# First-level sums of W1 and W2 moved to the first row's QKV stage, second-level sums of W1 called over the whole second one

## The chip, the cores and the metric

The kernel runs on one core of a Trainium2 chip. The metric is the time of one execution on the device, in microseconds. Before the change it was 2320.35 us, the median of 3 runs that lay between 2318.24 and 2321.5 us. The numbers of the trace come from one further execution, taken with the hardware profiler.

## What is computed

The reference is one block of a transformer with modulation by a condition (a DiT block), in fp32. x comes as (2, 2048, 512); each of its two rows is one sequence of 2048 tokens with causal attention over 16 heads of 32.

```
mod = silu(condition) @ Wada + bada
sh_a, sc_a, gt_a, sh_m, sc_m, gt_m = split(mod, 6)
xm = layernorm(x, g1, be1) * (1 + sc_a) + sh_a
x  = x + gt_a * attention(xm, Wqkv, Wproj, bproj)       # causal
xm = layernorm(x, g2, be2) * (1 + sc_m) + sh_m
h  = gelu(xm @ W1 + b1)                                 # W1: 512 x 2048
x  = x + gt_m * (h @ W2 + b2)                           # W2: 2048 x 512
```

## The kernel before

**Stages.** The program is written out by hand, stage after stage. A head computes the modulation from Wada and normalises the first tokens. Then come, for row 0, a QKV stage, an attention phase (line 541) and a projection phase (from line 1004); the same three for row 1; and last the MLP of both rows together.

**QKV stage.** `Qkv.run` (line 856) goes through four groups of 512 tokens. A group has 12 steps: eight tiles `ps_qk` of queries and keys and four tiles `ps_v` of values, each four matmuls of 128x512. Ahead of a group, its rows of x are loaded on SyncE (line 781), VectorE takes their statistics (line 215) and normalises them (line 263). Between the matmuls of these steps stand the score matmuls of the first attention units and the maxima that VectorE takes of them (lines 456 and 461). After step n of group g the stage calls `also(g, n)`, which is where the weight sums are put into the program's order. The row 0 stage has its `also` at line 1175, the row 1 stage at line 1228.

**Sums of weights.** The MLP does its two products by a scheme of seven products in place of eight (Strassen's, in Winograd's form), at two levels: seven outer ones of seven inner ones. The weights' side of it is made ahead of the MLP, on GpSimd, with scratch memory in DRAM between the levels.

*First level*, class `Quarters` (line 898). There are 16 pieces, 0 to 7 of W1 and 8 to 15 of W2. `step()` (line 924) issues the store of the piece before, takes a room, issues four loads of 128 KB (line 940) and four sums of 128x256 (line 922); the store (line 911) of 896 KB goes to `w1d` or `w2d`. A room holds one piece; where rooms come in pairs, two pieces share a buffer. Loads, sums and store are all on GpSimd: its DMAs go through the software queue, which is GpSimd's own.

*Second level of W1*, class `FirstLayer` (line 972). It reads `w1d` back, one load of 1024 KB (line 968) for each of seven outer products, makes four sums of 128x512 (line 963), and stores 1792 KB to `w1e` (line 996). Its buffer "w49" has two rooms; the first call issues two loads, and each later call the sums and the store of one room and the load of the next. The second-level sums of W2 are made in the MLP itself. SyncE reads `w1e` in the MLP.

**Where these calls stand before the change.** In the first row's stage the even steps of the last group each call `quarters.step()`: six pieces, 0 to 5. Their rooms are the buffer "wada", one buffer, two pieces to a fill. It holds Wada's last parts before, so it is free only after PE has used them for the last modulation. In the second row's stage the odd steps call `quarters.step()` until the last piece is stored (pieces 6 to 15, in the "w49" buffers), and from there on the even steps call `late.step()`.

**What sets the order.** Each engine works through its instructions in the program's order, and each instruction waits for the data and the buffer that it needs. The calls in `also` place GpSimd's work in GpSimd's own order only: behind the last GpSimd instruction of the code ahead of them, and ahead of the causal selects (line 602) and the sums of exponentials (line 623) of the attention units. Nothing ties a call to the matmul step that it stands behind, except the buffer it has to wait for. In the head GpSimd has two clears and the broadcasts of `bada`; in the QKV stages it has little else than these weight sums. The pool of tiles "qkv0" (variable `qp`) lives as long as the first stage.

Of the kernel before, what the change touches and what calls it, by code (L numbers as in the profile page):

```python
# [8 lines left out]
F32 = mybir.dt.float32  # L9
# [8 lines left out]
P = 128  # L18
# [9 lines left out]
def dit_block_kernel(  # L28
# [39 lines left out]
    C = D // P  # L68
# [5 lines left out]
    MTT = MT // P  # L74
    NG = T // MT
# [8 lines left out]
    def pool(name, bufs=1, **kw):  # L84
        return tc.tile_pool(name=name, bufs=bufs, reuse_waits="tile", **kw)
# [119 lines left out]
    def act(ins):  # L205

        return tc.keep_in_program_order(ins)
# [561 lines left out]
    class Qkv:  # L769
# [41 lines left out]
        def group(self, g, hp, between, among):  # L811
# [32 lines left out]
            for t in range(MTT):  # L844
# [9 lines left out]
                n += 1  # L854

        def run(self, hp, also):

            row = self.row
            for g in range(NG):

                def between(n):
                    if g + 1 < NG:
                        if n == 0 and g + 1 not in self.xts:
                            self.load_x(g + 1)
                        if n in (5, 8):
                            self.norm(g + 1, n // 8)()
                    elif n == 8:

                        row.rows(0)
                        act(nc.scalar.activation(first, eps, AF.Exp))  # L870
                    also(g, n)
# [22 lines left out]
    piece = 7 * C // 2 * P  # L894
# [172 lines left out]
    with pool("wada") as wp, pool("qkv0") as qp, pool(  # L1067
# [16 lines left out]
        def load_wada(s0, s1):  # L1084
            w = wp.tile([P, 2, C, D], F32, tag="wada", name="wada")
            if s0 % 3 == 2:
                mr = modr
            else:
                mr = wp.tile([P, D], F32, tag="mr", name="mr")
                nc.gpsimd.memset(mr, 0.0)  # L1090
            for n, s in enumerate((s0, s1)):
                nc.gpsimd.dma_start(
                    mr[n * HD : n * HD + B, :],
                    bada[s * D : (s + 1) * D].partition_broadcast(B),
                )
            for k in range(C):
                for n, s in enumerate((s0, s1)):
                    nc.sync.dma_start(w[:, n, k, :], wada_v[:, k, s * D : (s + 1) * D])
            wada[s0] = w, mr
# [12 lines left out]
        def modulation(s0):  # L1112

            w, mr = wada.pop(s0)
            ps = ps_sp.tile([P, D], F32, tag="s", name="ps_mod")
            for k in range(C // 2):  # L1120
                for half in range(2):
                    for n in range(2):
                        at = (2 * half + n) * HD
                        kk = half * C // 2 + k
                        mm(
                            ps[at : at + HD, :], sc[:, kk, :], w[:, n, kk, :],
                            start=(k == 0), stop=(k == C // 2 - 1),
                        )

            def columns():  # L1130
                nc.vector.tensor_tensor(mr, ps, mr, ALU.add)
                if s0 % 3 == 2:
                    return
                ps_t = ps_sp.tile([P, C, 2, B], F32, tag="s", name="ps_modt")
                for k in range(C):
                    mm(
                        ps_t[:, k], mr[:, k * P : (k + 1) * P], pickc,
                        start=True, stop=True,
                    )
                nc.vector.tensor_copy(  # L1140
                    mod[:, s0 : s0 + 2], ps_t.rearrange("p c s b -> p s c b")
                )

            return columns

        def scale_shift(a, c, r_g, r_be, shift, scale):

            for dst, r in ((a, r_g), (c, r_be)):
                nc.vector.scalar_tensor_tensor(
                    dst, mod[:, scale], 1.0,  # L1150
                    col(r, C).unsqueeze(2).to_broadcast([P, C, B]),
                    ALU.add, ALU.mult,
                )
            nc.vector.tensor_tensor(c, c, mod[:, shift], ALU.add)
# [17 lines left out]
                modulate((k, k + 1))  # L1172
        act(nc.vector.tensor_copy(pick, pickc.unsqueeze(3).to_broadcast([P, 2, B, P])))

        def also(g, n):

            if g == NG - 1 and n % 2 == 0:
                quarters.step()
            if g == 0 and n == 2:
                load_wada(2, 5)  # L1180
            elif g in (1, 2) and n == 3:
                qkv.columns = modulation(g + 1)
            elif g in (1, 2) and n == 4:
                qkv.columns()
                if g == 1:
                    load_wada(3, 4)
                else:
                    scale_shift(a2, c2, r_g2, r_be2, 3, 4)

        quarters = Quarters()  # L1190
        with pool("hl0") as hp:

            def rooms():

                w = wp.tile([P, 2 * C * D], F32, tag="wada", name="w7")
                return [w[:, k * piece : (k + 1) * piece] for k in range(2)]

            quarters.more_rooms = rooms
            qkv.run(hp, also)
            quarters.store()  # L1200
# [5 lines left out]
    with pool("qkv1") as qp, pool("ps_qkv1", bufs=6, space=PSUM) as ps_mm:  # L1206
        qkv = Qkv(row, qp, ps_mm)
        qkv.xts[0] = past.next_s

        def between(n):  # L1210
            if n == 6:
                qkv.load_w(nc.gpsimd)

            if n < MTT:
                qkv.stats(0, n, True)
            if n in (5, 8):
                qkv.norm(0, n // 8)()
            if n == 8:
                qkv.load_x(1)
            if n >= NT - MTT:  # L1220
                qkv.stats(1, n - (NT - MTT), True)

        project_phase(past, ps_mm, between)

        with pool("hl1") as hp:
            late = FirstLayer(hp)

            def also(g, n):
                if quarters.at <= FC:
                    if n % 2 == 1:  # L1230
                        quarters.step()
                elif n % 2 == 0:
                    late.step()

            def rooms():
                w = hp.tile([P, 7, C * P], F32, tag="w49", name="w7", bufs=2)
                w = w.rearrange("p n d -> p (n d)")
                return [w[:, k * piece : (k + 1) * piece] for k in range(2)]

            quarters.more_rooms = rooms  # L1240
            qkv.run(hp, also)
            assert quarters.at >= FC and late.at == 7 and not late.rooms
# [682 lines left out]
```

## Time and profile before

| what | us |
|---|---|
| median of 3 runs | 2320.35 |
| profiled execution | 2323.13 |
| its span | 2321.4 |
| head, up to the first QKV matmul | 18.46 |
| row 0: QKV stage | 194.99 |
| row 0: attention | 529.0 |
| row 0: projection | 60.4 |
| row 1: QKV stage | 195.5 |
| row 1: attention and projection | 599 |
| MLP | 724 |

The times of the stages are read from the trace, from the first matmul of one stage to the first of the next. The page of the profile gives first the busy time of each engine, then the span in forty slices, the DMA queues, and the chain of work that ended last; a row of the trace tells when an instruction began, how long it took, on what engine and line, out of which tile into which, and in square brackets how long its engine stood idle before it and which engine's result ended that (`<-DVE mx L456`: VectorE's tile mx, made in line 456). A row of a stretch tells begin and end, length, the busy time of PE, its weight loads, VectorE, ScalarE and GpSimd, the granted clock, the busy share of the DMA engines and GB/s. The row of a DMA shows the time of its issue on its queue, and the time to landing is given for a line as a group.

### The profile page before, as it was taken

The numbers are of one execution on the slowest core, as the hardware profiler recorded it, in microseconds if no ns is written. First come the engines' busy times: TensorE is split into PE (matmuls) and PEld (weight loads), VectorE is DVE, ScalarE is ACT, GpSimd is POOL, SyncE is SP. The second block draws the span as 40 slices with busy tenths as digits, with TensorE's granted clock in tenths as the row PEclk, the third lists the DMA queues.
The fourth block names the chain that finished last, engine by engine and source line by source line (L and its number), as shares of the span: only waits on it lengthen the run. The fifth ranks groups of instructions, "written<-read, shape, count | busy, mean of one in ns | idle before, by whom it ended". The sixth has DMA issues, their size and how long they took to land. (4 is left out here: it accounts for less than half of the span.)

```text
span 2321.4 us, 33398 instructions
## 1 busy us (share of the span) xinstructions
PE 2270.8 (98%) x12141; PEld 1388.8 (60%) x12141; DVE 1582.5 (68%) x3117; ACT 914.6 (39%) x1744; POOL 1290.9 (56%) x1036
## 2 busy tenths in 40 slices
PE   8999999999999999999999999999999999999998
PEld 4455545455544444555455554446888888888887
DVE  3366776777666735677667777555896876877787
ACT  2112555555565021155555554622332152251230
POOL 1052987878793663478788886653764602602510
PEclk9999999999999999999999999999999999999999
DMA  7577216151233799981522404265375554654643
GB/s 257 185 243 204 55 28 133 29 119 47 74 115 127 241 297 298 320 235 24 113 48 48 100 24 134 81 206 205 118 279 200 199 186 146 212 173 151 216 143 116
DMA packets 118524, 355.60 MB, mean 153 GB/s; under 512 B 14496, under 2 KB 15052, under 8 KB 103640
## 3 DMA queue, kind: packets, MB, share of 16 engines
q1 hardware_dynamic: 107040, 293.64, 41.9%
q0 software_dynamic: 10944, 59.28, 7.0%
q8 instruction: 96, 1.57, 0.3%
q14 instruction: 68, 0.56, 0.1%
q10 hardware_dynamic: 376, 0.55, 0.1%
HBM read 253.80 MB, written 107.48 MB: 156 GB/s over the span
## 5 line engine op out<-in xcount | busy, mean ns | idle before, releaser
L593 ACT ACTIVATE e<-st 128x512 f32<-128x512 f32 (+1 forms) x1152 | 573.1, 579 | 411.6 <-PE st L203 350.5
L461 DVE TENSOR_REDUCE mx<-s 128x1 f32<-128x512 f32 x604 | 408.0, 687 | 185.0 <-PE s L203 183.6
L623 POOL TENSOR_TENSOR ee<-ee,e 128x1024 f32<-128x1024 f32 x212 | 498.8, 2385 | 8.3 <-ACT e L593 8.3
L203 PE MATMUL s<-kst,qst 128*128 128x512 f32 (+3 forms) x1032 | 466.5, 453 | 15.9 <-DVE mx L461 6.3
L203 PE MATMUL st<-qst,kst 128*128 128x512 f32 (+3 forms) x1280 | 410.1, 387 | 0.0
L203 PE MATMUL ps_a<-sum,room 128*128 128x256 f32 x1504 | 357.4, 382 | 6.6 <-DVE c L1409 3.8
L203 PEld LDWEIGHTS ps_a<-sum,room 128*128 128x128 f32 x1504 | 281.5, 190 | 56.0 <-issue 8.7
L203 PE MATMUL o<-e,vv 128*32 128x512 f32 (+3 forms) x2560 | 300.8, 539 | 0.8 <-POOL e L602 0.8
L203 PEld LDWEIGHTS s<-kst,qst 128*128 128x128 f32 x1032 | 194.5, 189 | 174.0 <-DVE mx L461 58.6
L456 DVE CUSTOM_DVE_ANT_0 junk<-s,causal 128x512 bf16<-128x512 f32 (+3 forms) x428 | 209.2, 489 | 126.2 <-PE s L203 118.7
L203 PEld LDWEIGHTS st<-qst,kst 128*128 128x128 f32 x1280 | 227.5, 188 | 96.8 <-issue 66.7
L623 POOL TENSOR_TENSOR ee<-e 128x1024 f32<-128x1024 f32 x84 | 198.4, 2384 | 130.5 <-ACT e L593 130.4
L203 PE MATMUL ps_qk<-xmT,wqkv 128*128 128x512 f32 x512 | 240.5, 597 | 1.8 <-DVE xmT L263 1.8
L602 POOL TENSOR_SCALAR_AFFINE_SELECT e<-e 128x256 f32<-128x256 f32 x256 | 103.8, 436 | 107.2 <-ACT e L593 74.2
L203 PEld LDWEIGHTS ps_qk<-xmT,wqkv 128*128 128x128 f32 x512 | 94.2, 190 | 97.7 <-issue 91.4
L1637 POOL TENSOR_TENSOR c<-c,h 128x512 f32<-128x512 f32 x40 | 58.2, 1474 | 160.8 <-ACT c L1635 160.8
L203 PE MATMUL ps_b<-sum,room 128*128 128x256 f32 x608 | 143.6, 379 | 0.0
L203 PEld LDWEIGHTS ps_b<-sum,room 128*128 128x128 f32 x608 | 115.0, 190 | 15.4
L203 PE MATMUL ps_v<-wqkv,xmT 128*128 128x512 f32 x256 | 122.3, 594 | 0.0
L203 PEld LDWEIGHTS o<-e,vv 128*32 128x32 f32 x2560 | 60.8, 108 | 101.1 <-issue 83.4
L203 PE MATMUL st<-fold,sel 32*128 32x512 bf16 (+1 forms) x1152 | 116.1, 372 | 3.6 <-DVE mhl L482 2.6
L461 DVE TENSOR_REDUCE mx<-st 128x1 f32<-128x512 f32 x164 | 112.7, 687 | 4.9 <-PE st L203 2.7
(179 smaller groups left out, 2869.6 us busy)
## 6 DMA issues: line engine op xcount, KB each, us to landing
qst<-q SPq DMA_DIRECT2D x128, 256.0 KB
room<-w1e SPq DMA_DIRECT2D x28, 1024.0 KB
kst<-k SPq DMA_DIRECT2D x24, 1024.0 KB
room<-w1e SPq DMA_DIRECT2D x28, 768.0 KB
room<-w2e SPq DMA_DIRECT2D x21, 1024.0 KB
q<-hl SPq DMA_DIRECT2D x32, 512.0 KB
k<-hl SPq DMA_DIRECT2D x32, 512.0 KB
room<-w2e SPq DMA_DIRECT2D x21, 768.0 KB
```

What stands on the lines that cost most here:

```text
L203: return tc.keep_in_program_order(nc.tensor.matmul(*args, **kw))
L456: nc.vector.tensor_tensor_reduce(junk[:, :w], s[:, :w], causal[:, QB - w :], 1.0, MASKED, ALU.add, ALU.max, m,)
L461: nc.vector.tensor_reduce(m, s[:, :w], axis=AX.X, op=ALU.max)
L593: act(nc.scalar.activation(e[:, h % 2, :w], sts[h][:, :w], AF.Exp))
L602: nc.gpsimd.affine_select(d, d, pattern=[[0, 2], [1, P]], compare_op=ALU.is_ge, fill=0.0, base=0, channel_multiplier=-1,)
L623: act(engine.tensor_tensor(dst, x, y, ALU.add))
L1637: nc.gpsimd.tensor_tensor(c, c, piece_of(base, i, t, pair), ALU.add)
```

## The change

Two calls of `also` are rewritten. Neither the tiles nor the sums are changed, only in which room and at which place of GpSimd's order they are made.

In the first row's stage the 48 steps are numbered through (`at`). `free` is 29, the step behind the last modulation's use of Wada. Ahead of it, steps 9, 13, 17, 21 and 25 each make one piece, 0 to 4, in a room of its own from the pool `qp` (tag "w7", one buffer, so piece after piece) and issue its store at once. From step 29 on, each odd step makes a piece, 5 to 14, in the pairs of the "wada" buffer: five fills of it, where there were three. In the second row's stage, one piece is left (15); then `late.step()` is called at each step whose number leaves 2 when divided by 5, nine calls from step 7 on, where it was called at each even step after the pieces.

```diff
+        free = 2 * (C * 2 + MTT) + 5
+
         def also(g, n):
 
-            if g == NG - 1 and n % 2 == 0:
+            at = g * (C * 2 + MTT) + n
+            if at < free:
+                if at >= 9 and at % 4 == 1:
+                    quarters.rooms = [qp.tile([P, piece], F32, tag="w7", name="w7")]
+                    quarters.step()
+                    quarters.store()
+            elif at % 2 == 1:
                 quarters.step()
             if g == 0 and n == 2:
                 load_wada(2, 5)
...
             def also(g, n):
+                at = g * (C * 2 + MTT) + n
                 if quarters.at <= FC:
                     if n % 2 == 1:
                         quarters.step()
-                elif n % 2 == 0:
+                elif at % 5 == 2:
                     late.step()
```

## The prediction

> **What bounds the kernel now.** I read the page first, then the stretches by stage, then the waits and the order in time around the places where the matmul engine stands still.
>
> ```profile
> PE 2270.8 (98%) x12141; PEld 1388.8 (60%) x12141; DVE 1582.5 (68%) x3117; ACT 914.6 (39%) x1744; POOL 1290.9 (56%) x1036
> ```
>
> PE is occupied for 98% of the span of 2321.4 us, so some 50 us of the whole program are open idle time, and the work that the change moves (GpSimd sums of weights and their transfers) is on none of PE's instructions. It can only act where it makes PE wait, or stops PE from waiting. The next table is three of the stretches, with busy time by engine in the order PE, PEld, DVE, ACT, POOL, then granted clock, DMA share and GB/s: the head up to the first QKV matmul, the first row's QKV stage and the second row's.
>
> ```profile
> 0.00:18.46 18.46, 8.09 (x41) 4.76 (x41) 8.69 (x32) 3.68 (x6) 6.17 (x20) 1.00 0.89 300
> 18.46:213.45 194.99, 194.94 (x570) 95.22 (x571) 101.30 (x248) 38.57 (x69) 40.62 (x55) 1.00 0.68 217
> ...
> 802.80:998.30 195.50, 190.74 (x533) 93.80 (x532) 99.65 (x240) 36.85 (x67) 102.47 (x130) 0.99 0.93 310
> ```
>
> The first row's stage loses 0.05 us of PE; the second row's loses 4.76 us and some clock, with DMA at 0.93 instead of 0.68. In order of time, those 4.76 us are two stalls (PE rows), and the second is followed by 3.41 us at half clock (stretch row):
>
> ```profile
> 855.55 0.44 PE L203 MATMUL s<-kst,qst 128*128 128x384 f32 x1 [1.57 <-DVE mx L456]
> ```
> ```profile
> 902.83 0.50 PE L203 MATMUL s<-kst,qst 128*128 128x512 f32 x1 [3.17 <-DVE mx L461]
> ```
> ```profile
> 904.31:907.72 3.41, 3.41 (x7) 1.37 (x5) 1.72 (x4) 0.60 (x1) 0.00 (x0) 0.50 1.08 333
> ```
>
> So the stage has 1.57 + 3.17 + 3.41 x 0.5 = **6.45 us** to give, and no other stage is touched from that side. DVE is named, but DVE itself had waited for the next group's rows of x:
>
> ```profile
> 851.64 0.69 DVE L215 BATCH_NORM_STATS2 stat<-x 128x6 f32<-128x512 f32 x1 [3.27 <-DMA x<-in_x_dram]
> ```
> ```profile
> 842.34 3.18 SPq L781 DMA_DIRECT2D x<-in_x_dram  x4
> ```
>
> x is asked for at 842.34 and its second statistics still wait for it at 851.64, 9.3 us later. It comes late, its statistics and four subtractions then run in one piece, and the maxima of the scores wait behind them on DVE. PE has two banks for scores and stops. Over the stage DVE waits 13.7 us for x, in the first row's stage 2.8 us; that is the measure of how much the software queue's transfers press on SyncE's:
>
> ```profile
> DVE stat L215 <- DMA x<-in_x_dram: 13.7, 6, 4.7
> ```
> ```profile
> DVE stat L215 <- DMA x<-in_x_dram: 2.8, 2, 2.2
> ```
>
> **The change part by part.** Nine of the ten pieces of the second row's stage go to the first row's, and the order on PE, DVE, ACT and SyncE stays the same but for buffers. GpSimd's queue does not look at the clock: its instructions wait only for their own transfers and buffers, wherever the text places the call. Three places matter.
>
> *Head, +1.5 us.* Piece 0 has a room of its own, so its four loads go out right behind GpSimd's first four small ones. Until 18.46 us the DMA engines are busy 0.89, and the head ends on them:
>
> ```profile
> 12.39 0.18 PEld L203 LDWEIGHTS ps_mod<-wada,sc 128*32 128x32 f32 x4 [0.51 <-DMA wada<-in_L_cond_Wada_dram]
> ```
> ```profile
> 18.46 20.87 PE L203 MATMUL ps_qk<-xmT,wqkv 128*128 128x512 f32 x48 [1.78 <-DVE xmT L263]
> ```
> ```profile
> w<-in_L_cond_W_dram POOLq DMA_DIRECT2D x64, 128.0 KB, 5.5
> w1d<-w POOLq DMA_DIRECT2D x8, 896.0 KB, 7.1
> ```
>
> Wada feeds the modulation, which feeds xmT, which releases the first QKV matmul. 4 x 128 KB at the head's 300 GB/s are 1.7 us put in front of the rest of Wada. Bounds: nothing (they land behind Wada) and 2.5 us (at the 204 GB/s of a slow stretch below); I take 1.5. Pieces 1 to 4 follow one by one, each some 14 to 20 us (loads, 4 sums, a store that must land), and are done before 127 us. They fall in a stage at DMA share 0.68 whose DVE waits only 2.8 us for x: 0, at most 2 us if one store meets the x of the third group.
>
> *First attention, +2.6 us.* Pieces 5 to 14 go in five pairs through the room of the Wada buffer, which comes free where it did before. Before, there were three:
>
> ```profile
> 127.29 5.05 POOL L940 DMA_DIRECT2D w<-in_L_cond_W_dram  x7 [108.70 <-DMA kst<-k]
> ...
> 149.96 4.95 POOL L940 DMA_DIRECT2D w<-in_L_cond_W_dram  x7 [4.20 <-DMA w1d<-w]
> ...
> 157.26 2.32 POOL L922 TENSOR_TENSOR w<-w 128x256 f32<-128x256 f32 x3 [0.96 <-DMA w<-in_L_cond_W_dram]
> ...
> 164.16 1.06 POOL L911 DMA_DIRECT2D w1d<-w  x1 [0.30 <-POOL w L922]
> 169.44 4.95 POOL L940 DMA_DIRECT2D w<-in_L_cond_W_dram  x7 [4.22 <-DMA w1d<-w]
> ...
> 185.13 1.07 POOL L911 DMA_DIRECT2D w1d<-w  x1 [1.06 <-issue]
> ```
>
> The pairs start 22.67 and 19.48 us apart, and each must wait until the last pair's stores have landed. The landing of a store (the row is that of line 911 as a group) takes from its issue 4.7 us in quiet stretches, 8.9 in the median:
>
> ```profile
> DMA to landing us min/median/max: 4.7/8.9/12.4
> ```
> ```profile
> 835.98 2.15 POOL L940 DMA_DIRECT2D w<-in_L_cond_W_dram  x4
> ```
>
> The third pair lands at 185.13 + 8.9 = 194.0. A pair in quiet time: the second one took 165.22 - 149.96 = 15.26 us to the end of its last issue. The last pairs are of W2, whose issue takes 2.15 / 4 = 0.54 us against 4.95 / 7 = 0.71, so 8 x 0.17 = 1.4 less; without the 0.96 of waiting it is 12.9. Then 3.6 us to land and 0.6 to the next start. Pair four starts at 194.6, pair five at 211.7 and leaves GpSimd at **224.6**. Behind it in the same queue stand the causal selects of the first attention unit, two of them (2.28 / 6 = 0.38 us each in the row below) ahead of PE's first product with values:
>
> ```profile
> 222.83 1.07 PE L203 MATMUL o<-e,vv 128*32 128x512 f32 x8
> ```
> ```profile
> 1001.13 2.28 POOL L602 TENSOR_SCALAR_AFFINE_SELECT e<-e 128x256 f32<-128x256 f32 x6
> ```
>
> 224.6 + 0.8 + 0.1 of handing over - 222.8 = 2.6 us (after a head of 1.5 both ends move alike). Bounds: 0 if the pairs are 2.6 us quicker, 13.8 if the last two take the first one's 22.67 and 18.5. The key load of the next head group on SyncE now waits for the same room; it needs 27 us at 204 GB/s and its first reader comes at 269.21, so from 228.2 it lands at 255: covered by 14 us, nothing.
>
> ```profile
> 214.00:241.00 27.00, 25.90 (x180) 14.40 (x180) 19.56 (x42) 15.75 (x33) 13.23 (x13) 1.00 0.98 204
> ```
> ```profile
> 269.21 0.22 PE L203 MATMUL s<-kst,qst 128*128 128x128 f32 x1
> ```
>
> The Trainium skill, "TensorE: Matmul & The Clock Gate", section "What's actually happening", puts the fall to half rate after at least one idle window of about 3.4 us. By that rule a stall of 2.6 us costs no clock and the sum stays. The rows above show 3.17 us of idleness followed by 3.41 us at 0.50, and none at 1.57, so the limit here is lower, between the two; if it were passed, 1.7 us more.
>
> *Second QKV stage, -2.2 us.* The second-level rooms are said to be spread, one call in five. But GpSimd runs ahead: before, the seven rooms took from 902.19 to 1000.54, each waiting for the store of the room before.
>
> ```profile
> 902.19 0.59 POOL L968 DMA_DIRECT2D w<-w1d  x1
> ...
> 1000.54 0.58 POOL L996 DMA_DIRECT2D w1e<-w  x1 [0.30 <-POOL w L963]
> ```
> ```profile
> w1e<-w POOLq DMA_DIRECT2D x7, 1792.0 KB, 7.8
> ...
> w<-w1d POOLq DMA_DIRECT2D x7, 1024.0 KB, 7.7
> ```
>
> After the one piece left (2.15 us of issues, a few us of landing, four sums, one store) they start some 10 us into the stage and need 98, so they end near 910, so both x loads (the stalls at 854 and 900) still meet them. Per us that is more traffic than the pieces were: 7 x 2816 KB in 98 us, some 205 GB/s, against 10 x 1408 KB in 99 us, 145 GB/s. But it comes in bursts, one room in 14 us, with gaps while the sums run. I count one stall as relieved (the mean of 1.57 and 3.17 + 1.71, so 3.2) and 1.0 lost at the other: -2.2. Bounds: -6.45 (both gone) and +4.3 (rival B). GpSimd's shorter tail at 1001 gives nothing: the six selects there ran late already, and PE did not wait.
>
> Sum: 1.5 + 2.6 - 2.2 = **+1.9 us** on the profiled execution's 2323.13, which lies 2.8 above the median of the runs shown; on that median of 2320.35 it gives **2322.3**.
>
> **The rivals.** What a measurement of this kernel can tell from no change is about 0.2%, 4.6 us.
>
> *A, slower: the room's chain is too long.* The fourth and fifth pair take as long as the first (22.67, then 18.5 to its last issue). GpSimd ends at 194.6 + 22.7 + 18.5 = 235.8, PE stands 13.8 us and loses 1.7 of clock: 1.5 + 13.8 + 1.7 - 2.2 = +14.8, **2335.1**. For it: two of three pairs took that long. Against: the transfers of SyncE that slowed them thin out after 190 us. It decides from GpSimd's end at about 227.3 on, 2.7 us later than I expect.
>
> *B, slower: x starves in the second stage.* The two queues share the DMA engines by packets, and the software queue's are large there:
>
> ```profile
> q0 software_dynamic: 83, 1.19, 97.2%
> q1 hardware_dynamic: 53, 0.08, 11.1%
> ```
>
> That is 965 to 968 us: 14 KB a packet against 1.5 KB, and 15 times the bytes. Over the 9.3 us of an x load the extra 55 to 60 GB/s are 0.53 MB, at the 1.27 MB in 3 us that both reached together 1.3 us; both stalls grow by 1.3, and the first now loses 1.7 of clock too: +4.3 in place of -2.2, so 1.5 + 2.6 + 4.3 = +8.4, **2328.8**. The Trainium skill, "DMA: Bandwidth & Descriptors", section "Queues, rings and completion order", has each engine take one packet of each waiting queue in turn; by that rule the share of SyncE is 1.5 in 15.5, and the row agrees.
>
> *C, faster: it does what it says.* The bursts miss both x loads, piece 0 hides behind Wada and the pairs end by 222: -6.45, **2313.9**. For it: the first stage had no stall with six pieces in it. Against: all three must hold, and nothing in GpSimd's queue paces it.
>
> **How the numbers follow.** Within 0.2% (the forecast, with parts of each rival): 0.45. A 0.22 and B 0.16 make slower 0.38; C makes faster 0.17. The range leaves out the far half of A and the end of C: 2315 to 2332.
>
> **What would show it.** In the changed profile: the first QKV matmul near 20.0 instead of 18.46; five starts of line 940 after 127 us, the last near 213, and PE's first product waiting for GpSimd's select for 1 to 5 us; seven rooms ending near 910 and not 990; one of the two stalls on x smaller. I am wrong if the rooms do reach the end of the stage, if the head does not move, or if GpSimd ends before 222 or after 228 (less the head's shift).

## The result, and the profile after

The changed kernel takes 2340.15 us in the median of 7 runs (2326.43 to 2343.42), against 2320.35 us: the ratio is 1.0072, with a 95% interval of 1.0053 to 1.0091. The prediction was 2322.3 with a range up to 2332, so the time lies outside it, on the slow side. The profiled execution took 2339.0 us.

PE's order is the same in both kernels, so each of its 12141 matmuls can be set beside itself in the trace of before. The shift of the first matmul of each stage gives where the time went:

| stage | predicted | found |
|---|---|---|
| head | +1.5 | +1.5 |
| row 0: QKV stage | 0 | -0.1 |
| row 0: attention | +2.6 | +7.9 |
| row 0: projection | 0 | -0.6 |
| row 1: QKV stage | -2.2 | +10.6 |
| row 1: attention and projection | 0 | 0.0 |
| MLP | 0 | -3.5 |
| sum | +1.9 | +15.8 |

The MLP's -3.5 is not the change's: the profiled execution of before had a stall of 2.33 us at 1834.94 with a half-clock stretch behind it, and the one of after has none. None of the experiments touches the MLP either: one of them has a stall of this kind (2.34 us at 2201.67), the others have none. Without the MLP the shifts add up to 19.3 us, close to the 19.8 between the medians.

First the page's line of busy times, then the stretches by stage, as they were shown of before (head, first QKV stage, second QKV stage). The last two rows end 0.75 and 0.23 us behind the matmul that ended those of before, which adds nothing to what is read from them:

```profile
PE 2274.5 (97%) x12141; PEld 1388.5 (59%) x12141; DVE 1588.7 (68%) x3117; ACT 915.1 (39%) x1744; POOL 1292.7 (55%) x1036
```
```profile
0.00:19.95 19.95, 9.51 (x41) 4.29 (x41) 8.68 (x32) 3.68 (x6) 9.03 (x24) 1.00 0.86 304
19.95:215.59 195.64, 195.23 (x571) 95.33 (x572) 102.97 (x251) 39.31 (x70) 81.98 (x114) 1.00 0.83 265
811.64:1017.84 206.20, 193.02 (x534) 95.41 (x533) 106.35 (x239) 37.10 (x67) 48.90 (x51) 0.97 0.72 239
```

The first stage took nine more pieces and loses nothing: GpSimd is busy 82 us there where it was 41, DMA 0.83 where it was 0.68. The second stage has less traffic than before, DMA 0.72 against 0.93, and still idles 206.20 - 193.02 = 13.2 us of PE where it idled 4.8. Its stalls and the stall of the first attention, in PE's order of time, and then the stretches at half clock that lie around them:

```profile
230.24 1.42 PE L203 MATMUL o<-e,vv 128*32 128x512 f32 x4 [5.94 <-POOL e L602]
```
```profile
865.53 0.69 PE L203 MATMUL s<-kst,qst 128*128 128x384 f32 x1 [2.82 <-DVE mx L456]
```
```profile
921.60 0.80 PE L203 MATMUL s<-kst,qst 128*128 128x512 f32 x1 [10.36 <-DVE mx L461]
```
```profile
227.10:233.92 6.82, 3.68 (x16) 1.11 (x16) 0.00 (x0) 0.00 (x0) 5.18 (x11) 0.50 0.55 211
865.39:868.80 3.41, 3.27 (x5) 1.72 (x6) 3.37 (x7) 0.11 (x1) 3.24 (x3) 0.50 0.98 384
916.59:926.83 10.24, 5.23 (x8) 2.72 (x9) 6.63 (x9) 0.60 (x1) 5.38 (x5) 0.50 0.98 377
```

The clock costs half of PE's busy time in each: 1.8 us in the attention, 1.6 + 2.6 in the second stage (1.7 before). With the idle time, 5.94 + 1.8 is the attention's 7.9 but for 0.2, and 13.2 - 4.8 + 4.2 - 1.7 = 10.9 the second stage's 10.6.

What VectorE did ahead of the stall of 10.36 us (its rows), what GpSimd did at that time, and the same four normalisations before the change:

```profile
904.00 0.69 DVE L215 BATCH_NORM_STATS2 stat<-x 128x6 f32<-128x512 f32 x1 [2.50 <-DMA x<-in_x_dram]
...
912.17 8.18 DVE L244 TENSOR_SCALAR x<-x,mv,rstd 128x512 f32<-128x512 f32 x4
920.27 0.68 DVE L831 SCALAR_TENSOR_TENSOR hl<-ps_qk,hl 128x512 fp32r<-128x512 f32 x1
920.87 0.67 DVE L461 TENSOR_REDUCE mx<-s 128x1 f32<-128x512 f32 x1
```
```profile
910.34 5.12 POOL L963 TENSOR_TENSOR w<-w 128x512 f32<-128x512 f32 x4
915.76 0.58 POOL L996 DMA_DIRECT2D w1e<-w  x1 [0.30 <-POOL w L963]
916.36 5.11 POOL L963 TENSOR_TENSOR w<-w 128x512 f32<-128x512 f32 x4
```
```profile
899.36 2.22 DVE L244 TENSOR_SCALAR x<-x,mv,rstd 128x512 f32<-128x512 f32 x4
```

The normalisation is line 244: it takes the mean from x and multiplies by the inverse deviation, from SBUF (the on-chip memory of the engines) to SBUF. Line 263, which the description of the stage names for it, scales and shifts the transposed tiles on their way out of PSUM (the memory that matmuls write to). x was there; the four normalisations took 8.18 us. Four of them take 1.9 us where GpSimd does not add. VectorE counts as busy in these 8 us, waits for nothing that the profile shows, and the maxima for PE's scores stand behind them. That a wait is booked as duration is what made it easy to miss; the group rows show it, since the same shape has another mean than it had before (the stage's group of before, then of after):

```profile
L244 DVE TENSOR_SCALAR x<-x,mv,rstd 128x512 f32<-128x512 f32 x12 | 7.6, 684 | 0.1
```
```profile
L244 DVE TENSOR_SCALAR x<-x,mv,rstd 128x512 f32<-128x512 f32 x12 | 14.4, 1248 | 0.1
```

**Two theories** were set against each other. L, lock: VectorE's normalisation and GpSimd's sums exclude each other, and a normalisation waits until a sum is over. X, late x: the stalls come from x landing late among GpSimd's transfers, as the prediction had it. The Trainium skill, "SBUF — State Buffer", section "Who interferes with whom", has a rule for L: VectorE's fast form of a tensor-scalar operation uses a pair of ports that it shares with GpSimd, and whichever comes first holds the pair for its whole instruction. It also says that an operation with at most one input in SBUF, outside that form, does not contend. The trace agrees: line 263, the same kind of operation out of PSUM, takes 532 to 544 ns for all 12 in this stage, and the statistics of line 215 take 659 to 695 ns, also those that ran beside sums (line 263 at 878.98, 0.54 us; line 215 at 910.58, 0.66 us).

### The profile page after: what moved, and what is told of

Read it like the earlier page. It is cut to its first block, busy times and chain, and to the rows that moved or that the text cites. A ratio compares the mean times of both kernels' runs of the same rounds, so it can differ in the third digit from the quotient of the medians.

```text
span 2337.3 us, 33411 instructions
## 1 busy us (share of the span) xinstructions
PE 2274.5 (97%) x12141; PEld 1388.5 (59%) x12141; DVE 1588.7 (68%) x3117; ACT 915.1 (39%) x1744; POOL 1292.7 (55%) x1036
## 3 DMA queue, kind: packets, MB, share of 16 engines
q8 instruction: 96, 1.57, 0.3%
```

## The experiments

Times are medians beside those of the kernel before on the same chip; the ratio is to before, in brackets its 95% interval.

**The normalisation in another order of elements.** The first test of L tried to get VectorE out of its fast form.

```diff
...
+            to, of = xn, xt
+            if turn:
+                to, of = [v.rearrange("p (k d) -> p d k", k=2) for v in (xn, xt)]
             nc.vector.tensor_scalar(
-                xn, xt, mv[:, n, 0:1], rstd[:, n : n + 1], ALU.subtract, ALU.mult
+                to, of, mv[:, n, 0:1], rstd[:, n : n + 1], ALU.subtract, ALU.mult
             )
```

> The changed kernel with one edit: VectorE's normalisation of x in the second row's QKV stage (line 244) reads and writes the same 512 elements in another order (two halves interleaved), so that it no longer runs in its fast form of 0.54 us. Theory L (lock): in the changed kernel the four normalisations of the last group took 8.4 us in place of 2.2 because they stood while GpSimd's sums of 5.1 us ran; in the slow form, some 0.67 us each, they no longer wait for GpSimd. Then the stall of 10.36 us falls to about 5, the one of 2.82 to about 1.5, and the time from 2340 to about 2333. Theory X (late x): the stall comes from x landing late among GpSimd's transfers; then it stays at 10 us or grows by 0.5, and the time stays at 2340.

2342.08 us against 2321.4, ratio 1.0090 [1.0073, 1.0106]. Neither expectation holds as it was written: the stall grew to 14.09 us, where L has it fall to about 5 and X has at most 0.5 us more.

```profile
914.57 9.32 DVE L247 TENSOR_SCALAR x<-x,mv,rstd 128x512 f32<-128x512 f32 x4
```

The operation became slower (0.79 us where nothing disturbs it) and its four took 9.32 us beside GpSimd's sums, as before. So this slower order of elements is no way out of the lock. The run says nothing against X: VectorE waited 9.34 us for x there, ahead of the normalisations. The Trainium skill, "VectorE: DVE Perf Modes", section "Mode 2×_2P — use both read ports for one tensor", asks only that the single source and the destination lie in SBUF and that their outermost dimension be even (or odd and equal in both); the turned form, with 256, still meets that. The trace agrees in so far as the turned form is held up by GpSimd's sums too (4.77 us for one of the four).

**The rooms tied to their steps.** Ahead of each call GpSimd copies one column of what ScalarE wrote in that step (`self.mark`, set after each tile of the stage). This is called the spread kernel below.

```diff
...
                 elif at % 5 == 2:
+                    mark = qp.tile([P, 1], F32, tag="mark", name="mark")
+                    act(nc.gpsimd.tensor_copy(mark, qkv.mark))
                     late.step()
```

> The changed kernel with the calls of the second level really tied to their steps: ahead of each, GpSimd copies one column of what ScalarE wrote in that step. GpSimd now comes to the rooms at steps 7, 12, 17 ... 42, so the last store is issued near 985 and not 922. If spreading alone is what was missing (the change as it was meant), both stalls go and the time is about 2327. Theory L: the room of step 17 has its sums at the step at which the second group's normalisation is called, the one of step 27 just ahead of the third's; stalls of 3 to 5 us stay at both places, 2336 to 2340. Theory X: the stores of steps 12 and 22 are in flight when the two loads of x are issued, so both stalls stay, each like before the change or larger, 2333 to 2340.

2327.12 us against 2321.4, ratio 1.0028 [1.0017, 1.0039]. The time is the one forecast for spreading alone, but the stalls are not gone. The rooms now reach to 1000 and not 922. The first stall is as long as before the change (1.64 us, 1.57 before); the second is shorter (1.85, 3.17 before) and no half-clock stretch follows it:

```profile
866.64 0.44 PE L203 MATMUL s<-kst,qst 128*128 128x384 f32 x1 [1.64 <-DVE mx L456]
```
```profile
912.61 0.50 PE L203 MATMUL s<-kst,qst 128*128 128x512 f32 x1 [1.85 <-DVE mx L461]
```

The second stage is 3.2 us shorter than before the change, where the changed kernel's is 10.6 longer. So the spreading that the change describes does help, and the changed kernel does not do it. The eight normalisations take 0.54 us each here: no sums stood beside them. That is with L, but x also came sooner, so it settles nothing.

**Thirteen pieces in the first row's stage, three in the second.**

```diff
-            elif at % 2 == 1:
+            elif at % 2 == 1 and quarters.at < 13:
                 quarters.step()
```

> The changed kernel with 13 pieces in the first row's stage (four fills of the Wada room and not five) and three in the second. GpSimd leaves the fourth pair at about 210, ahead of the first select of attention. If the fifth pair is what PE's first product with values waited for, the stall of 5.94 us and its half-clock stretch go: 8.3 us less up to 240. If it was another wait (the key load behind the room), it stays. In the second stage the rooms start 12 us later; by theory L the stalls there change in size by several us either way, as the sums meet the normalisation or not, by theory X they stay. 2332 with 5 either way.

2326.9 us against 2321.4, ratio 1.0021 [1.0006, 1.0036], just below the 2327 to 2337 expected. GpSimd is free when the first select comes, and PE has no stall there:

```profile
210.76 1.07 POOL L911 DMA_DIRECT2D w2d<-w  x1 [0.30 <-POOL w L922]
219.50 0.40 POOL L602 TENSOR_SCALAR_AFFINE_SELECT e<-e 128x256 f32<-128x256 f32 x1 [7.67 <-ACT e L593]
```

The first attention is now as long as before the change (PE's shift against before is +3.29 at its start and +3.35 at its end). In the second stage a stall of 8.13 us stays, and this one is mostly X's: VectorE waits 9.50 us for x, its four normalisations then take 3.1, which is 1.2 more than undisturbed.

```profile
903.41 0.69 DVE L215 BATCH_NORM_STATS2 stat<-x 128x6 f32<-128x512 f32 x1 [9.50 <-DMA x<-in_x_dram]
```

**Piece 0 held back.** The clear was put on two columns of the room that no load writes.

```diff
...
+            if at == 0:
+                own.append(qp.tile([P, piece], F32, tag="w7", name="w7"))
+                act(nc.vector.memset(own[0][:, :2], 0.0))
...
```

> The changed kernel with piece 0 held back: VectorE clears two columns of its room at the first QKV step, so its four loads can't go out before some 22 us. If these loads are what made the head longer, the first QKV matmul is back at 18.5 from 19.95 (1.0 to 1.5 us less); five pieces one after the other still end by 115 us, so the rest is unchanged: 2339. If the head's shift is chance, the first QKV matmul stays near 20.

2340.44 us against 2321.4, ratio 1.0086 [1.0066, 1.0107]. The loads went out at 5.37 as before and only the sums were held, so the first QKV matmul stayed at 19.78. So holding the sums does not give the head back, and the loads are not tested here; that comes with the kernel of three corrections below. The rest of the time is as in the changed kernel.

**Sums moved onto the normalisation.** The spread kernel with its rooms at other steps.

```diff
...
-                elif at % 5 == 2:
+                elif at in (7, 13, 19, 24, 29, 34, 38, 42):
...
```

> The spread kernel (rooms tied to steps 12, 17, 22, 27 ...) with its rooms moved by one to three steps, to 13, 19, 24, 29, 34, 38 and 42, so that GpSimd's sums of steps 13 and 24 begin near 863 and 908, where VectorE normalises the third and the fourth group's x (866.7 and 909.5 in the spread kernel, each of the eight in 0.54 us, stalls of 1.64 and 1.85). The transfers are as many and hardly nearer to the loads of x. Theory L: the normalisations stretch to 2 to 4 us each where the sums run, and one or both stalls grow to 5 us or more; 2331 to 2335. Theory X: no sum matters; stalls stay within 1 us of 1.64 and 1.85, and the time stays at 2327.

2325.28 us against 2321.37, ratio 1.0018 [1.0009, 1.0028]. The sums missed: the room of step 24 added from 905.97 on, and x had come sooner, so the fourth group was normalised by 905.7 in 0.54 us each. The stall there vanished. Neither forecast of the stalls holds, as no sums ran beside the fourth group's normalisations, and nothing is decided; it led to a test that moves no transfer ahead of the stall.

**Eight idle sums beside the normalisation.** The base of this pair is the kernel of three corrections, told last. The sums are of a small buffer with itself, and nobody reads them; the two kernels differ in the room behind which they stand (`n` 2 or 5).

```diff
...
             act(nc.gpsimd.dma_start(w1e[n], room))
+            if n == 2:
+                for k in range(8):
+                    act(nc.gpsimd.tensor_tensor(self.idle, self.idle, self.idle, ALU.add))
             self.load()
...
```

> The kernel with three things put right and eight sums more on GpSimd, of a small buffer of their own with itself (128x512, 1.27 us each, no transfer, read by nobody), behind the store of the room of step 22: some 10 us from 892.5 to 902.7, over the normalisation of the fourth group's x (897.1 to 899.0, 0.54 us each, stall of 1.92). The next room's load comes 3 us later; no transfer is added. Theory L: the four normalisations are held, 2 us in the mean and the last one till the sums end, and the stall grows from 1.9 to 5 us or more; 2320 to 2322. Theory X: the stall stays at 1.9, 2316.

> The control to the kernel before it: the same eight sums behind the store of the room of step 37 (some 958 to 968), where VectorE normalises nothing. By both theories nothing changes: stalls as in the kernel with three things put right, 2316. If GpSimd's sums slow other work of VectorE too, PE shows a new stall near 960.

Beside the normalisation: 2320.02 us against 2320.3, ratio 1.0004 [0.9993, 1.0015]. The control: 2315.67 us, ratio 0.9982 [0.9973, 0.9992]. The sums and the normalisations of the first kernel, and PE's stall:

```profile
892.29 9.12 POOL L1001 TENSOR_TENSOR idle<-idle 128x512 f32<-128x512 f32 x8
```
```profile
896.17 4.34 DVE L244 TENSOR_SCALAR x<-x,mv,rstd 128x512 f32<-128x512 f32 x4
```
```profile
901.76 0.80 PE L203 MATMUL s<-kst,qst 128*128 128x512 f32 x1 [3.71 <-DVE mx L461]
```

And of the control, whose sums ran from 954:

```profile
894.76 1.92 DVE L244 TENSOR_SCALAR x<-x,mv,rstd 128x512 f32<-128x512 f32 x4
```
```profile
897.93 0.50 PE L203 MATMUL s<-kst,qst 128*128 128x512 f32 x1 [0.90 <-DVE mx L461]
```

4.34 us against 1.92 for the same four instructions, in kernels that differ only in where GpSimd's idle sums stand. PE's stall is 3.71 against 0.90; 2.4 of the 2.8 us between them are the normalisations, the rest is x, which came 0.4 later in that execution (counted from the start of the stage). The medians differ by 4.4 us, half clock behind the stall included. L is shown, and X's forecast of no change fails. The stall's size was put too high: 5 us was expected, 3.7 found, as these normalisations got in between one sum and the next and did not wait for the last.

Whether they get in depends on the gap between the sums, as far as the records of single instructions show it. An idle sum reads what the last one wrote and starts 0.08 us behind its end; a normalisation came through after each of them and took 1.26 us. Of the four sums of a room (changed kernel, from 916.36) the first three follow each other without a gap, and only the fourth starts 0.07 us behind. The last normalisation of the group stood from 916.12 through all three and took 4.23 us.

**The lock taken out of the changed kernel.** One copy of a column, which makes the sums of the sixth room wait until the fourth group is normalised.

```diff
                 elif at % 5 == 2:
+                    if at == 37:
+                        mark = qp.tile([P, 1], F32, tag="mark", name="mark")
+                        act(nc.gpsimd.tensor_copy(mark, qkv.xts[NG - 1][MTT - 1][:, :1]))
                     late.step()
```

> The changed kernel with one copy of 128x1 more on GpSimd, ahead of the sums of the sixth room: it reads the last tile of the fourth group's x after VectorE has normalised it, so these sums (and those of the last room behind them) can't run beside that normalisation. All transfers up to there are untouched, so x lands as late as in the changed kernel. Theory L: the four normalisations take 1.9 us in place of 8.2, the stall of 10.36 falls to about 4, the long half-clock stretch behind it to one of 3.4: 2331 to 2333. Theory X: the stall stays at 9 to 10.5, 2340.

2335.23 us against 2320.5, ratio 1.0061 [1.0043, 1.0079].

```profile
916.11 0.18 POOL L1244 COPY mark<-x 128x1 f32<-128x1 f32 x1 [4.18 <-DVE x L244]
```
```profile
914.13 1.92 DVE L244 TENSOR_SCALAR x<-x,mv,rstd 128x512 f32<-128x512 f32 x4
```
```profile
917.29 0.80 PE L203 MATMUL s<-kst,qst 128*128 128x512 f32 x1 [5.81 <-DVE mx L461]
```

The normalisations are back at 1.92, the stall falls by 4.55 us and the median by 4.9. That is L's direction and most of its size (it has the stall at about 4 and the time at 2331 to 2333); X's, 9 us or more, fails. What stays, 5.81 against the 3.17 of before, is put down to late x: here the first normalisation came 15.5 us after x was asked for at 898.62, before the change 13.6 (899.36 - 885.74). No run takes this rest away by itself.

```profile
885.74 4.25 SPq L781 DMA_DIRECT2D x<-in_x_dram  x4
```

**The normalisation on ScalarE.**

```diff
...
+            act(nc.scalar.activation(less[:, 0:1], rstd1[:, n : n + 1], AF.Copy, scale=-1.0))
+            act(nc.scalar.activation(
+                less[:, 1:2], mv1[:, n, 0:1], AF.Copy, scale=less[:, 0:1]))
+            act(nc.scalar.activation(
+                xt, xt, AF.Identity, bias=less[:, 1:2], scale=rstd1[:, n : n + 1]))
```

> The changed kernel with the normalisation of the second row's later groups moved from VectorE (line 244) to ScalarE, with two small columns made on ScalarE for it; the scheduler moves some statistics on VectorE with it. Theory L: nothing of VectorE's is held by GpSimd's sums any more; the stall of 10.36 falls by the some 6 us that the four normalisations took too long, to about 4, and the time to 2333. Theory X: x lands as late as before, and the stall stays at 9 us or more, 2340.

2345.37 us against 2321.37, ratio 1.0102 [1.0087, 1.0117]. The stall behind the maxima does fall to 3.34, as L has it, but PE now waits for ScalarE's tiles wherever a group is normalised, and the time is the longest of all, beyond both forecasts. As the order of work moved too, the run is no clean test of either theory.

```profile
834.11 0.33 PE L211 MATMUL ps_xt<-ident,x 128*128 128x128 f32 x1 [1.95 <-ACT x L822]
...
925.48 0.50 PE L203 MATMUL s<-kst,qst 128*128 128x512 f32 x1 [3.34 <-DVE mx L465]
```

**Three corrections together.** Piece 0's four loads held by a clear of columns that they write, 13 pieces, and the rooms tied to steps.

```diff
...
+                act(
+                    nc.vector.memset(
+                        own[0].rearrange("p (n d) -> p n d", n=7)[:, 2:6, :2], 0.0
+                    )
+                )
...
-            elif at % 2 == 1:
+            elif at % 2 == 1 and quarters.at < 13:
...
-                elif at % 5 == 2:
+                elif at in (8, 12, 17, 22, 27, 32, 37, 42):
+                    mark = qp.tile([P, 1], F32, tag="mark", name="mark")
+                    act(nc.gpsimd.tensor_copy(mark, qkv.mark))
                     late.step()
```

> The changed kernel with three things put right: piece 0's loads held until the first QKV step (VectorE clears two columns of each of the four parts that they write), 13 pieces in the first row's stage and three in the second, and the rooms tied to steps 12, 17, 22, 27, 32, 37 and 42. If the three losses are independent: the head is back at 18.5, no stall in the first attention, and the second stage's stalls are those of the spread kernel (1.6 and 1.9, no half clock), 3.5 us better than before the change: 2317. If the load of piece 0 was not what made the head longer, 1 to 3 us more.

2316.31 us against 2321.37, ratio 0.9974 [0.9965, 0.9984]: faster than both kernels, if by a quarter of a percent against before, and within 1 us of what was expected. None of the three losses is left, and the head's was piece 0's loads: in the five traces of kernels that hold them the first QKV matmul starts at 17.80 to 18.75, in the eight that do not, at 19.75 to 20.45.

```profile
0.00:18.42 18.42, 8.26 (x42) 4.77 (x42) 8.66 (x32) 3.69 (x6) 6.19 (x20) 1.00 0.89 314
18.42:215.07 196.65, 195.81 (x571) 95.11 (x571) 102.56 (x252) 39.23 (x70) 85.14 (x118) 1.00 0.84 265
803.38:995.59 192.21, 190.29 (x533) 94.32 (x532) 98.48 (x239) 37.06 (x67) 62.02 (x77) 0.99 0.81 271
```

The second stage idles 1.9 us where it idled 4.8 before and 13.2 after the change. Its stalls are not quite the expected ones: the first is gone, and the second, 1.92 us, is followed by half clock.

**The same with no room's store beside the last x.**

```diff
-                elif at in (8, 12, 17, 22, 27, 32, 37, 42):
+                elif at in (8, 12, 17, 26, 30, 34, 38, 42):
```

> The kernel with three things put right, its rooms moved to steps 12, 17, 26, 30, 34, 38, 42: no store of a room is in flight from the issue of the fourth group's x (884) to its normalisation (899). Theory X for what is left of the stalls: the stall of 1.92 at 900 goes or falls below 1; 2314.5. If it is set by SyncE's own traffic (keys, queries and x together), it stays, 2316.

2317.58 us against 2320.3, ratio 0.9989 [0.9979, 0.9999]. The stall in the trace is 0.83, but the control above, with the rooms at the old steps, has 0.90. The two can't be told apart, and the median is no better: inconclusive.

**x on GpSimd's queue.** The loads of x go out at step 9, on GpSimd, ahead of the rooms (`self.load_x(g + 2, nc.gpsimd)`).

> As the kernel with three things put right, and the loads of x for the third and fourth group are issued on GpSimd's queue at step 9 of the group before the one that needs them now (they wait for their buffers only), ahead of the rooms, instead of on SyncE behind the stores of queries and keys; rooms at steps 12, 15, 22, 26, 33, 37, 41, clear of the normalisations. Theory X says that what is left of the stalls is late x: both go, 6.5 us better than before in this stage, 2314. Theory L alone says that with no sums beside the normalisations nothing more is won: 2317.

2326.24 us against 2321.37, ratio 1.0017 [1.0008, 1.0027]. The loads for the third group went out at 838 and its stall is gone. Those for the fourth had to wait in GpSimd's queue behind a room's load until 883.7, and the scheduler had put their statistics earlier on VectorE, so VectorE stood 14.6 us for them and PE 9.46:

```profile
891.21 0.69 DVE L215 BATCH_NORM_STATS2 stat<-x 128x6 f32<-128x512 f32 x1 [14.60 <-DMA x<-in_x_dram]
```

Both forecasts fail (2314 and 2317), and not because x was late: its statistics start at 891.21, in the kernel of three corrections at 893.07. What moved is their place. They stand ahead of a maximum that PE's scores need, where they stood behind it before. With normalisations of 0.55 us, a wait for x placed there costs as much as the lock and late x together did.

## Why the prediction was wrong

*Head, +1.5: right.* Found 1.5, and the kernel with piece 0's loads held starts at 18.42.

*First stage at no cost: right.* The five single pieces were made by 104 us, and the stage lost nothing.

*First attention, +2.6: the mechanism was right, two terms of the sum were mis-sized.* GpSimd's rows of the pairs:

```profile
171.52 3.76 POOL L940 DMA_DIRECT2D w<-in_L_cond_W_dram  x7 [4.19 <-DMA w2d<-w]
...
186.64 1.07 POOL L911 DMA_DIRECT2D w2d<-w  x1 [0.94 <-POOL w L922]
197.50 3.77 POOL L940 DMA_DIRECT2D w<-in_L_cond_W_dram  x7 [9.79 <-DMA w2d<-w]
...
209.48 1.07 POOL L911 DMA_DIRECT2D w2d<-w  x1 [0.30 <-POOL w L922]
216.72 3.77 POOL L940 DMA_DIRECT2D w<-in_L_cond_W_dram  x7 [6.17 <-DMA w2d<-w]
...
228.68 1.07 POOL L911 DMA_DIRECT2D w2d<-w  x1 [0.30 <-POOL w L922]
229.69 2.97 POOL L602 TENSOR_SCALAR_AFFINE_SELECT e<-e 128x256 f32<-128x256 f32 x8
```

A pair's own time was forecast as 12.9 and is 13.0, twice. The waits for the stores to land were put at 8.4 and 4.2 and are 9.79 and 6.17, together 3.4 more; GpSimd ended at 229.7 where 224.6 and the head's 1.5 make 226.1. So PE waited 5.94, and half clock took 1.8 more. The prediction put the clock's limit between 1.57 and 3.17 us of idleness and then left it out for 2.6. The trace of before already had shorter waits with half clock behind them, 2.04 us at 1424.34 and 2.33 at 1834.94. This stage is between the forecast and rival A.

*Second QKV stage, -2.2: the step that failed.* "I count one stall as relieved ... and 1.0 lost at the other." The rooms ran ahead as was said, from 820 to 922. But neither stall was relieved: the first grew by 1.25 us with 1.6 of half clock behind it, the second by 7.19 with 2.6 of half clock where it was 1.7. VectorE's waits for x grew from 13.7 us to

```profile
DVE stat L215 <- DMA x<-in_x_dram: 16.9, 5, 6.6
```

which is the side of rival B. The first stall is x alone, as its maxima stand ahead of the normalisation (865.19 against 865.60). For the second, the forecast looked at GpSimd's DMAs alone and never at its sums as something that VectorE could wait for. The rooms' sums moved from behind the normalisations (from 912.85 on, before the change) to beside them, and a room's are 5.1 us in one piece where a piece's are 3.0. Of the 7.2 us by which the longer stall grew, the copy that takes out the lock gives back 4.6; the other 2.6 are put down to late x in that execution's trace. In the changed kernel's own, the first normalisation came 1.2 us later after x was asked for than before, and the four took 6.0 longer; so the two traces split the loss 1.4 us apart.

*Rivals.* A was half right. B was right in sign and place, and for the first stall in size (1.3 forecast, 1.25 found); the larger mechanism is missing from it. C asked for rooms that are spread; the kernel with rooms tied to steps shows that part of it was possible.

*What could have been seen.* The trace of before held the sign. In its view of line 244 the shortest and the longest of one shape differ by thirteen times, at 761 to 772 us, where GpSimd adds in the projection (the longest, 7.03 us, beside five sums of 1.27 us that follow each other):

```profile
L244 DVE TENSOR_SCALAR qst<-qst,mv,rstd x12: 532/1205/7026, 761.3 to 1572.0; 128x512 f32<-128x512 f32 x12
```

Left open: the changed kernel's runs spread over 17 us, those of before over 4 beside them (over 12 in 19 runs on another chip). That the sums meet the normalisation in some executions and miss it in others would explain it; only one execution of it was traced, so it is not shown.

## What to carry to other kernels

Where work moves to an engine's idle time, look at what the other engines do at that time, and not at its transfers alone: compare the shortest and the longest duration of one shape, since here the wait for GpSimd's sums was booked as busy time of VectorE. A call's place in the text spreads nothing on a queue that waits only for its own transfers; a one-column copy that reads what the paced stage has just written does, and in the second stage it decided here between 10.6 us lost and 3.2 won. And size a chain of dependent transfers by the landing times at the end of its stretch, with the price of half clock once PE's wait comes near 2 us.

## What the runs showed of the hardware

Half clock follows shorter waits than the 3.17 us that the prediction had seen. In the kernel of three corrections 1.92 us of idleness at 900.24 were followed by a stretch at half clock:

```profile
901.40:904.82 3.42, 3.42 (x8) 1.73 (x6) 1.28 (x5) 0.60 (x1) 0.00 (x0) 0.50 0.84 294
```

1.64 and 1.85 us in the spread kernel were not, nor were 1.97 at 865.51 in the kernel with the lock taken out. The wait ahead of the first QKV matmul is 1.77 or 1.78 us in all fourteen traces, and in five of them half clock follows. So it is not the length of one wait alone that decides.

Where the wait falls counts too. Within each trace all half-clock stretches begin on one grid of 3.413 us; before the change, for instance, those at 904.31, 1426.55 and 1836.14 are 153 and 120 steps apart. They are one step long or several: two behind the 5.94 us of the attention, three behind the 10.36, five behind the 14.09 of the reordered normalisation. The 1.92 us above lie whole within one step (897.99 to 901.40), while the 1.85 and the 1.97 are split by the end of one and leave at most 1.50 and 1.72 in a step. That fits idle time counted step by step, but it is not a full rule: 1.91 us within one step were not followed by half clock in the kernel with ScalarE (from 898.12), and 1.32 were before the change (the step from 1423.13).
